# Layer 0's preparation in a four-layer network on one Trainium2 core: batch statistics from row tiles, another queue and layout for the first weights, per-channel factors through transposed rows, and a bias table split before it is spread

## The chip, the cores and the metric

The kernel runs on one core of a Trainium2 chip. A core has a matrix engine (TensorE, PE in the profile, its weight loads PEld), a vector engine (VectorE, DVE), a scalar engine (ScalarE, ACT), a general one (GpSimd, POOL) and a queue engine for transfers (SyncE, SP). Each runs its own instructions in the order in which they stand in its queue; semaphores order the engines against each other. SP, ScalarE and GpSimd can issue transfers (DMA) between the chip's memory and the on-chip memory. The metric is the device time of one execution in microseconds (us).

## The reference, cut to what matters

Four layers work on `x` of shape (4, 8, 512, 512), each as `x = x + layer(_gn(x))`, where `_gn` normalises over groups of planes. The change touches what is prepared for layer 0, a spiking attention block:

```python
T, B, N, D, H = (4, 8, 512, 512, 8)
def bn(x, g, b, m, v):
    return g * (x - m) * jax.lax.rsqrt(v + EPS) + b
q = heads(lif(bn(x @ Wq.T, bnq_g, bnq_b, bnq_m, bnq_v)))
k = heads(lif(bn(x @ Wk.T, bnk_g, bnk_b, bnk_m, bnk_v)))
v = heads(lif(bn(x @ Wv.T, bnv_g, bnv_b, bnv_m, bnv_v)))
scores = jnp.einsum('tbhnd,tbhmd->tbhnm', q, k) * scale
rel = pos[None, :] - pos[:, None] + (N - 1)
bias = bias_table[rel].transpose(2, 0, 1)
scores = scores + bias[None, None]
out = lif(einsum(scores, v) in token order)
out = out * gate_scale + gate_shift
out = lif(bn(out @ Wp.T, bnp_g, bnp_b, bnp_m, bnp_v))
```

`lif` steps a potential over the four time steps `t`, emits a spike where it reaches 1 and resets it. Layers 1 to 3 are convolutions of 13x13, 3x3 and 3x3.

## The kernel before

**Tiling.** Layer 0 works in 32 steps, one for each of 8 images and 4 time steps. A plane of 512 x 512 values is 1 MB; it is loaded in four transfers of 256 KB. `load_x` loads rows: four tiles of 128 partitions with 2 KB each, from six buffers (tag `x`). `load_quarters` loads the same plane into one tile `xq` for a transpose in blocks: each of its four transfers goes to 32 partitions, in pieces of 512 bytes; there is one buffer.

**Before the first step.** `load(0)` fetches `xq` of step 0, then `load_weights("v", nc.sync)` the weights `w_v` (1 MB, four transfers to 32 partitions each). `statistics` runs `bn_stats` (L431) over the two images of the first group: the first from `xq`, the second from rows (`xs`). `norm_of` combines them (L177 to L197) into a mean and a reciprocal deviation. `batch_norms` (L315 on) turns the batch norm's parameters into `a_half` and `c_half`, one value for each channel, laid along the partitions. Then `transpose` normalises `xq` in place (L618), transposes it (L480), and the projections begin (L499).

**Factors along the free axis.** The weights of v, k and the output are scaled by a factor for each output channel, which lies along the free axis. `along_free` brings it there: for each of four chunks it makes a diagonal matrix on VectorE (L336) and multiplies it by a matrix of ones on PE (L337). `prepare_in` uses it for v and k, `prepare_out` for the output's weights `wp`.

**Bias.** For each head the bias is a Toeplitz matrix. The kernel keeps it as three bf16 parts (`toep`), whose sum is the fp32 value, with 896 columns in 128 partitions. `prepare_bias` loads for each of 8 heads a table that is shifted by one element from partition to partition (L361, 448 KB), casts it reversed on ScalarE (L365), subtracts on VectorE (L366), casts (L367), subtracts on GpSimd (L368), and casts (L369). Its two scratch tiles have the tags `h_o` and `h_p`. The scratch of `bands1`, which prepares layer 1's bands (L726 to L757, `ps_band` at L741), takes tag `h_p` after it.

**Step loop.** Iteration `n` attends for step `n` and projects for step `n + 1`, in the order v, k, q (the q projection's potentials `v_q`, tag `v` with three buffers, go through ScalarE at L450). In iteration −1 only the projections of step 0 run, and then `prepare_bias`, `prepare_out`, `next_group` and `bands1`. Attention forms `ps_kv` (L515), for each of four head pairs `ps_a` (L527) and `ps_b` (L535, with `toep`), and then the potential `v_o` (L545 on ScalarE, L550 on VectorE). `project_out` (L562) uses the two parts of `wp`, which are made by L401, L405, L406 and L407.

**Order.** The program is written in one sequence. A planner puts the instructions into the engines' queues by priority in that sequence and by times that it expects, so a later instruction can stand ahead of an earlier one that has to wait. `tc.issue_after(op)` keeps what its block traces on `op`'s engine behind `op`. At run time each queue is strictly in order, and a transfer that has no free buffer or semaphore holds what stands behind it in its queue.

Of the kernel before, what the change touches and what calls it, by code (L numbers as in the profile page):

```python
# [34 lines left out]
F32 = mybir.dt.float32  # L35
# [8 lines left out]
P = 128  # L44
# [222 lines left out]
def layer0(  # L267
# [34 lines left out]


    def load_weights(n, engine):
        rows = i[f"wT_{n}"].rearrange("(q c a) e -> q a c e", c=NC, a=SQ)
        for q in range(P // SQ):
            engine.dma_start(wT[n][q * SQ : (q + 1) * SQ], rows[q])

    nc.scalar.dma_start(cols.rearrange("p a b -> p (a b)"), i["cols"])
    bn = cols[:, :16, :].rearrange("p (n s) c -> p n s c", s=4)  # L310
    ones = wpool.tile([P, P], F32, name="ones")
    nc.vector.memset(ones, 1.0)

    def batch_norms():

        neg_half = wpool.tile([P, 4, NC], F32, name="nh0")
        nc.vector.memset(neg_half, -0.5)
        nc.vector.tensor_scalar_add(a_half, bn[:, :, 3, :], EPS)
        nc.gpsimd.tensor_tensor(a_half, a_half, neg_half, op=ALU.pow)
        nc.vector.tensor_mul(a_half, a_half, bn[:, :, 0, :])  # L320
        nc.vector.tensor_scalar_mul(a_half, a_half, 0.5)
        c = c_half[:, :3, :]
        nc.vector.scalar_tensor_tensor(
            c, bn[:, :3, 2, :], -1.0, a_half[:, :3, :], op0=ALU.mult, op1=ALU.mult
        )
        nc.vector.scalar_tensor_tensor(
            c, bn[:, :3, 1, :], 0.5, c, op0=ALU.mult, op1=ALU.add
        )

    def along_free(cols):  # L330


        ps = ps_mm.tile([P, D], F32, tag="mm", name="ps_free")
        for c in range(NC):
            diag = work.tile([P, P], F32, tag="diag", name="diag", bufs=2)
            nc.vector.tensor_scalar_mul(diag, ident, cols[:, c : c + 1])  # L336
            nc.tensor.matmul(  # L337
                ps[:, c * P : (c + 1) * P], lhsT=ones, rhs=diag, start=True, stop=True
            )
        return ps  # L340

    def phases(x):
        return x.rearrange("p (v g) -> p g v", g=PH)

    def prepare_in(n):
        j = "qkvp".index(n)
        scale = along_free(a_half[:, j, :])
        for k in range(NC):
            nc.vector.tensor_mul(wT[n][:, k, :], wT[n][:, k, :], scale)
        return nc.scalar.mul(c_twice[n], along_free(c_half[:, j, :]), 2.0).ins  # L350

    def prepare_bias():


        n_u = toep[0].shape[2]
        table = i["table"]
        hankel = state.tile([P, 2, n_u], F32, tag="h_o", name="hankel")
        rest = state.tile([P, 2, n_u], F32, tag="h_p", name="rest")
        for h in range(H):
            src, r = hankel[:, h % 2, :], rest[:, h % 2, :]  # L360
            nc.scalar.dma_start(  # L361
                src, bass.AP(table.tensor, h * (2 * N - 1), [[1, P], [1, n_u]])
            )
            dst = [w[:, h, :] for w in toep]
            nc.scalar.copy(dst[0], src[:, ::-1])  # L365
            nc.vector.tensor_sub(r, src[:, ::-1], dst[0])  # L366
            nc.scalar.copy(dst[1], r)  # L367
            nc.gpsimd.tensor_sub(r, r, dst[1])  # L368
            nc.scalar.copy(dst[2], r)  # L369

    def load_out():
        wp32 = work.tile([P, NC, D], F32, tag="so", name="wp32")
# [3 lines left out]
    def prepare_out(wp32):  # L376
        gate_scale, gate_shift = cols[:, 16, :], cols[:, 17, :]

        shift = ps_1.tile([P, NC], F32, tag="misc", name="shift")
        for e in range(NC):  # L380
            for k in range(NC):
                nc.tensor.matmul(
                    shift[:, e : e + 1],
                    lhsT=wp32[:, k, e * P : (e + 1) * P],
                    rhs=gate_shift[:, k : k + 1],
                    start=k == 0,
                    stop=k == NC - 1,
                )
        c = c_half[:, 3, :]
        nc.vector.tensor_sub(c, shift, bn[:, 3, 2, :])  # L390
        nc.vector.tensor_mul(c, c, a_half[:, 3, :])
        nc.vector.scalar_tensor_tensor(c, bn[:, 3, 1, :], 0.5, c, op0=ALU.mult, op1=ALU.add)

        nc.scalar.mul(
            c_twice["p"].rearrange("p (g v) -> p g v", g=PH), phases(along_free(c)), 2.0
        )
        scale = work.tile([P, D], F32, tag="v", name="scale_p", bufs=3)
        nc.scalar.copy(scale, along_free(a_half[:, 3, :]))
        for k in range(NC):
            wp = work.tile([P, D], F32, tag="v", name="wp_k", bufs=3)  # L400
            nc.vector.scalar_tensor_tensor(  # L401
                wp.rearrange("p (g v) -> p g v", g=PH), phases(wp32[:, k, :]),
                gate_scale[:, k : k + 1], phases(scale), op0=ALU.mult, op1=ALU.mult,
            )
            nc.scalar.copy(wpT[0][:, k, :], wp)  # L405
            nc.vector.tensor_sub(wp, wp, wpT[0][:, k, :].bitcast(F32))  # L406
            nc.scalar.copy(wpT[1][:, k, :], wp)  # L407

    def load_x(b, t, name):
        got = []  # L410
        for c in range(NC):
            xt = xp.tile([P, D], F32, tag="x", name=f"{name}_{b}_{t}_{c}")
            nc.sync.dma_start(xt, x_in[t, b, c * P : (c + 1) * P, :])
            got.append(xt)
        return got
# [9 lines left out]
    def as_rows(xt):  # L425
        flat = xt.rearrange("p j f -> p (j f)")
        return [flat[:, c * D : (c + 1) * D] for c in range(NC)]
# [176 lines left out]
    def statistics(g, t, pair, xt):  # L604
        key = g, t
        if pair == 0:
            norms[key] = new_stats(g, t)
        count(xt, norms[key], pair)
        if pair == PAIR - 1:
            norms[key] = norm_of(g, t, norms[key])  # L610
# [12 lines left out]
    def load(n):  # L623
        if n <= last:
            xs[n] = load_quarters(*steps[n])
# [14 lines left out]
        image_bands(nc, bt, band, 0, r1[:, 0, 0:1], eye)  # L640
        return band, eye, x, bt

    load(0)
    load_weights("v", nc.sync)
    statistics(0, 0, 0, as_rows(xs[0]))
    statistics(0, 0, 1, load_x(1, 0, "xs"))
    batch_norms()
    for k in range(NC):
        transpose(0, k)
    with tc.issue_after(prepare_in("v")):  # L650
# [4 lines left out]
    for n in range(-1, last + 1):  # L655
        b, t = steps[max(n, 0)]
        if n >= 0:
            with tc.issue_after(did) if n == 0 else ExitStack():
                so = attend(spikes, t)
            residual = load_x(b, t, "xr")  # L660
            if n == last:
                head = start_layer1()
        if n + 1 <= last:
            spikes = new_spikes()
            g, j = divmod(n + 1, PAIR * T)
            if n >= 0:
                load(n + 2)
            if j == 2 and g > 0:
                norm1(g - 1, ps_1)
            if g == 0 and n >= 0 and n + 2 < T:  # L670
                statistics(0, n + 2, 0, as_rows(xs[n + 2]))
                statistics(0, n + 2, 1, load_x(1, n + 2, "xs"))
            if n >= 0:
                next_group(n)
        for a, name in enumerate("vkq"):
            for c in range(NC):
                if n + 1 <= last:
                    did = project_in(name, c, xns[n + 1], spikes, steps[n + 1][1])
                if (n, name, c) == (-1, "v", 0):
                    first += [prepare_in("k"), did, potentials[0]]  # L680
                    with ExitStack() as behind:
                        for op in first:
                            behind.enter_context(tc.issue_after(op))
                        load(1)
                        statistics(0, 1, 0, as_rows(xs[1]))
                        statistics(0, 1, 1, load_x(1, 1, "xs"))
                if n >= 0 and a < 2 and c % 2:
                    project_out(so, 2 * a + c // 2, residual[2 * a + c // 2], b, t)
                if a == 2 and c % 2:
                    transpose(n + 2, c // 2)  # L690
        if n + 1 <= last:
            del xns[n + 1]
        for k in range(2, NC):
            transpose(n + 2, k)
        if n < 0:
            with ExitStack() as behind:
                for op in first:
                    behind.enter_context(tc.issue_after(op))
                prepare_bias()
                prepare_out(load_out())  # L700
                next_group(n)
                bands1(tc, i, band1d, w_sum, eye, ps_mm, state)
            for name in "op":
                h_of[name] = state.tile([P, NC, N], F32, tag=f"h_{name}", name=f"h_{name}")
# [614 lines left out]
```

## Time and profile before

| what | value |
|---|---|
| median of 3 runs | 2932.97 us (2931.45 to 2935.19) |
| the profiled execution | 2934.12 us |
| its span, first to last instruction | 2932.3 us |
| PE busy | 2826.4 us (96%), 12,865 matmuls |
| VectorE busy | 2210.8 us (75%) |
| ScalarE busy | 551.0 us (19%) |
| GpSimd busy | 1036.6 us (35%) |
| read from and written to the chip's memory | 210.57 MB and 103.60 MB |

The profile gives for every instruction its start, its duration, its line in the kernel and what it waited for; times count from the start of the span. Its page shows the whole span in 40 slices of 73 us, with the busy share of each engine in tenths. Its other views can be cut to a stretch of time: busy time by stretch, instructions in order of time with the idle time ahead of each and what ended it, transfers by queue, and waits by engine. Busy times of PE are those of pipelined matmuls. "Granted clock" is the share of its full clock that PE was allowed.

### The profile page before, as it was taken

How to read it: one execution, taken by the hardware profiler on the slowest of the kernel's cores; microseconds unless marked ns; L12 is line 12 of the kernel's file. 1: busy time of each engine (PE TensorE's matmuls, PEld its weight loads, DVE VectorE, ACT ScalarE, POOL GpSimd, SP SyncE). 2: the span in 40 equal slices, each digit the busy share in tenths (PEclk: the TensorE clock that was granted, in tenths of full speed). 3: DMA queues.
4: the chain of work that ended last, by engine and by line, in shares of the span. 5: the costliest groups of instructions: out<-in, count | busy, mean ns of one | idle time of the engine just before them, and what ended most of it. 6: DMA issues, size and time to landing. Idle time of an engine off the chain costs nothing. (4 is left out here: it accounts for less than half of the span.)

```text
span 2932.3 us, 36617 instructions
## 1 busy us (share of the span) xinstructions
PE 2826.4 (96%) x12865; PEld 1302.0 (44%) x12865; DVE 2210.8 (75%) x3916; ACT 551.0 (19%) x860; POOL 1036.6 (35%) x1924
## 2 busy tenths in 40 slices
PE   6899999999999999999999999999999999589999
PEld 3454555554555544455455555455333333223334
DVE  7897788688779778868877886886655556887870
ACT  1300010011010001001000000110111111766664
POOL 3342233343234323323422433332211112676650
PEclk9899999999999999999999999999999999999999
DMA  7333322223222223222222122113878779698865
GB/s 182 100 81 80 73 59 66 72 71 78 64 66 66 73 76 70 59 66 66 73 66 51 45 59 51 52 44 87 224 194 222 207 200 242 145 212 214 221 171 147
DMA packets 323895, 322.10 MB, mean 110 GB/s; under 512 B 21431, under 2 KB 237183, under 8 KB 323599
## 3 DMA queue, kind: packets, MB, share of 16 engines
q1 hardware_dynamic: 261872, 237.39, 33.4%
q0 software_dynamic: 19776, 56.14, 6.0%
q10 hardware_dynamic: 42063, 26.23, 3.2%
q8 instruction: 101, 1.65, 0.3%
q14 instruction: 83, 0.68, 0.1%
HBM read 210.57 MB, written 103.60 MB: 107 GB/s over the span
## 5 line engine op out<-in xcount | busy, mean ns | idle before, releaser
L499 PE MATMUL ps_in<-w_v,xn 128*128 128x512 f32 x1024 | 459.2, 598 | 3.0 <-DVE xn L480 3.0
L499 PE MATMUL ps_in<-w_kq,xn 128*128 128x512 f32 x1024 | 450.1, 592 | 0.0
L815 PE MATMUL ps_conv<-x,bt 112*64 112x512 f32 x2048 | 445.0, 592 | 0.8 <-DVE v_p L467 0.8
L499 PE MATMUL ps_in<-xn,w_kq 128*128 128x512 f32 x1024 | 444.6, 592 | 0.0
L535 PE MATMUL ps_b<-toep,vtok 128*64 128x512 bf16 x3072 | 368.9, 384 | 1.0 <-DVE v_o L550 1.0
L475 POOL TENSOR_TENSOR h_v<-h_v,c_v 128x512 f32<-128x512 f32 x96 | 122.0, 1271 | 683.9 <-DVE h_v L474 658.2
L450 ACT ACTIVATE h_q<-v_q,c_half 128x512 f32<-128x512 f32 x96 | 69.2, 721 | 1473.6 <-DVE v_q L446 950.4
L584 POOL COPY x1s<-x1s 128x2 f32<-128x2 f32 (+1 forms) x1024 | 227.7, 277 | 272.3 <-DVE x1s L573 272.3
L562 PE MATMUL ps_out<-wp,so 128*128 128x512 f32 x1024 | 308.9, 444 | 0.0
L499 PEld LDWEIGHTS ps_in<-xn,w_kq 128*128 128x128 f32 x1024 | 194.3, 190 | 233.0 <-issue 223.2
L499 PEld LDWEIGHTS ps_in<-w_kq,xn 128*128 128x128 f32 x1024 | 194.2, 190 | 219.9 <-issue 204.7
L499 PEld LDWEIGHTS ps_in<-w_v,xn 128*128 128x128 f32 x1024 | 190.9, 191 | 218.4 <-issue 210.1
L815 PEld LDWEIGHTS ps_conv<-x,bt 112*64 112x64 f32 x2048 | 144.9, 135 | 290.2 <-issue 288.1
L1220 PE MATMUL ps_conv<-x,band_t 64*64 64x512 f32 x2040 | 251.4, 609 | 3.1 <-DVE band_t L1189 3.1
L535 PEld LDWEIGHTS <-vtok 128*64 128x64 bf16 x3072 | 176.0, 111 | 155.5 <-issue 7.0
L1083 POOL COPY u<-x 128x512 f32<-128x512 f32 (+1 forms) x172 | 211.7, 1266 | 91.8 <-issue 48.2
L562 PEld LDWEIGHTS ps_out<-wp,so 128*128 128x128 f32 x1024 | 192.6, 188 | 94.4 <-issue 58.1
L573 DVE SCALAR_TENSOR_TENSOR x1s<-v_p,xr 128x256 f32<-128x256 f32 x256 | 188.6, 777 | 13.1 <-DMA x<-x1s 2.3
L837 POOL DMA_DIRECT2D x<-xo x128 | 71.6, 566 | 314.0 <-ACT xo L822 299.7
L475 POOL TENSOR_TENSOR h_k<-h_k,c_k 128x512 f32<-128x512 f32 x96 | 123.3, 1284 | 135.9 <-DVE h_k L474 135.9
L822 ACT ACTIVATE xo<-ps_conv,off 128x512 f32<-128x512 f32 x128 | 87.9, 687 | 430.9 <-PE ps_conv L815 314.8
L1125 DVE SCALAR_TENSOR_TENSOR x<-ps_conv,inv,u 128x512 f32<-128x512 f32 (+1 forms) x172 | 121.3, 745 | 56.3 <-PE ps_conv L1118 29.0
(192 smaller groups left out, 3268.5 us busy)
## 6 DMA issues: line engine op xcount, KB each, us to landing
x<-x SPq DMA_DIRECT2D x64, 917.0 KB
x<-x SPq DMA_DIRECT2D x168, 256.0 KB
x<-x1s POOLq DMA_DIRECT2D x128, 262.0 KB, 2.7
xq<-in_x SPq DMA_DIRECT2D x128, 256.0 KB
xr<-in_x SPq DMA_DIRECT2D x128, 256.0 KB
out<-o SPq DMA_DIRECT2D x164, 192.0 KB
xs<-in_x SPq DMA_DIRECT2D x112, 256.0 KB
x<-xo ACTq DMA_DIRECT2D x128, 128.0 KB
```

The lines of the kernel that those rows point to most:

```text
L475: nc.gpsimd.tensor_add(h, h, c_twice[n])
L499: mm = nc.tensor.matmul(ps, lhsT=lhsT, rhs=rhs, start=k == 0, stop=k == NC - 1)
L535: nc.tensor.matmul(pb[two * DH : (two + 1) * DH, :], lhsT=v[:, c, h * DH : (h + 1) * DH], rhs=toep[z][:, h, u : u + N], start=c == 0 and z ...
L562: nc.tensor.matmul(ps, lhsT=so[:, k, c * P : (c + 1) * P], rhs=wpT[z][:, k, :], start=k == 0 and z == 0, stop=k == NC - 1 and z == 1,)
L573: nc.vector.scalar_tensor_tensor(own, v.rearrange("p (g v) -> p g v", g=PH)[:, two, :], 1.0, by_phase[:, two, :], op0=ALU.is_ge, op1=ALU.add,)
L584: nc.gpsimd.tensor_copy(x1[:, f, u : u + n], x1[:, fm, um - n + 1 : um + 1][:, ::-1])
L815: mm = nc.tensor.matmul(ps[q * M1 : (q + 1) * M1, :], lhsT=bt[:, z, :], rhs=xt[:, w0 : w0 + N_PS1, z : z + NV], start=z == 0, stop=z == SH ...
L822: nc.scalar.activation(xo[:, a, :], ps, AF.Identity, bias=off[:, t : t + 1])
L837: engine.dma_start(bass.AP(dst.tensor, dst.offset + (q * n_half * W1_OUT * B + b) * D + f * NV, [[B * D, W1_OUT], [W1_OUT * B * D, n_half] ...
L1083: nc.gpsimd.tensor_copy(u[:n_p, j, :].rearrange("p (v g) -> p v g", g=PH), x[:, j, :].rearrange("p (g v) -> p v g", g=PH),)
L1125: done["DVE"] = nc.vector.scalar_tensor_tensor(own, ps[:n_p, :], w["inv"][:n_p], u[:n_p, j, :], op0=ALU.mult, op1=ALU.add, accum_out=sums[ ...
L1220: mm = nc.tensor.matmul(ps[j][b * HALF : (b + 1) * HALF, :], lhsT=band[half, b, dx, :], rhs=x3[half, s0 + j, dx : dx + D], start=dx == 0, ...
```

## The change

Five things change. (1) `batch_norms` is traced first and returns its last operation. The statistics of both images of the first group come from row tiles, behind that operation on VectorE; `xq` of step 0 is traced after them. (2) The weights of v are loaded from ScalarE's queue and not from SP's, and each of the four transfers of any of these weights covers 128 partitions with 2 KB rather than 32 with 8 KB. (3) `along_free` takes rows that PE has transposed and ScalarE has copied (`as_rows_of`), and spreads them with a column of the identity, broadcast, as the stationary operand; the diagonals and the matrix of ones are gone. In `prepare_out` the scale is now traced ahead of `c`. (4) `split_bias` splits the table while it is compact, as 24 partitions of 341 values, on VectorE, and stores the three bf16 parts in the chip's memory. (5) `prepare_bias` loads each part, shifted by one element from partition to partition, for two heads at a time, and ScalarE copies it reversed into `toep`: 12 loads and 12 copies.

```diff
     def load_weights(n, engine):
-        rows = i[f"wT_{n}"].rearrange("(q c a) e -> q a c e", c=NC, a=SQ)
-        for q in range(P // SQ):
-            engine.dma_start(wT[n][q * SQ : (q + 1) * SQ], rows[q])
+        rows = i[f"wT_{n}"].rearrange("(q c a) e -> c q a e", c=NC, a=SQ)
+        for c in range(NC):
+            engine.dma_start(wT[n][:, c, :], rows[c])
...
+    def as_rows_of(cols):
+        n = cols.shape[1]
+        ps = ps_mm.tile([n, P], F32, tag="mm", name="ps_rows")
+        nc.tensor.transpose(ps, cols, ident)
+        rows = wpool.tile([4 * NC, P], F32, tag="rows", name="rows", bufs=2)
+        nc.scalar.copy(rows[:n], ps)
+        return rows[:n]
+
+    def along_free(rows, j):
+        n = rows.shape[0]
         ps = ps_mm.tile([P, D], F32, tag="mm", name="ps_free")
         for c in range(NC):
-            diag = work.tile([P, P], F32, tag="diag", name="diag", bufs=2)
-            nc.vector.tensor_scalar_mul(diag, ident, cols[:, c : c + 1])
+            at = NC * j + c
             nc.tensor.matmul(
-                ps[:, c * P : (c + 1) * P], lhsT=ones, rhs=diag, start=True, stop=True
+                ps[:, c * P : (c + 1) * P], lhsT=ident[:n, at : at + 1].to_broadcast([n, P]),
+                rhs=rows, start=True, stop=True,
             )
...
+    def split_bias():
+        n_e = n_h // 3
+        parts = tc.dram_tile([3, H * n_h], BF16, name="bias_parts")
+        src = state.tile([3 * H, n_e], F32, tag="h_o", name="bias_table")
+        nc.scalar.dma_start(src, bass.AP(i["table"].tensor, 0, [[n_e, 3 * H], [1, n_e]]))
+        part = state.tile([3 * H, 3, n_e], BF16, tag="h_p", name="bias_part")
+        for z in range(3):
+            nc.vector.tensor_copy(part[:, z, :], src)
+            if z < 2:
+                nc.vector.tensor_sub(src, src, part[:, z, :])
+        nc.scalar.dma_start(
+            bass.AP(parts.tensor, parts.offset, [[n_e, 3 * H], [H * n_h, 3], [1, n_e]]), part
+        )
+        return parts
+
+    def prepare_bias(parts):
+        for h in range(0, H, 2):
+            for z in range(3):
+                hankel = state.tile(
+                    [P, 2, n_u], BF16, tag="h_o" if (h + z) % 2 else "h_p", name="hankel"
+                )
+                nc.scalar.dma_start(
+                    hankel,
+                    bass.AP(
+                        parts.tensor, parts.offset + (z * H + h) * n_h, [[1, P], [n_h, 2], [1, n_u]]
+                    ),
+                )
+                nc.scalar.copy(toep[z][:, h : h + 2, :], hankel[:, :, ::-1])
...
+        scale = work.tile([P, D], F32, tag="v", name="scale_p", bufs=3)
+        nc.scalar.copy(scale, along_free(a_rows, 3))
 
         nc.scalar.mul(
-            c_twice["p"].rearrange("p (g v) -> p g v", g=PH), phases(along_free(c)), 2.0
-        )
-        scale = work.tile([P, D], F32, tag="v", name="scale_p", bufs=3)
-        nc.scalar.copy(scale, along_free(a_half[:, 3, :]))
+            c_twice["p"].rearrange("p (g v) -> p g v", g=PH), phases(along_free(as_rows_of(c), 0)), 2.0
+        )
...
-    load(0)
-    load_weights("v", nc.sync)
-    statistics(0, 0, 0, as_rows(xs[0]))
-    statistics(0, 0, 1, load_x(1, 0, "xs"))
-    batch_norms()
+    normed = batch_norms()
+    a_rows = as_rows_of(a_half.rearrange("p n c -> p (n c)"))
+    c_rows = as_rows_of(c_half[:, :3, :].rearrange("p n c -> p (n c)"))
+    load_weights("v", nc.scalar)
+    with tc.issue_after(normed):
+        for pair in range(PAIR):
+            statistics(0, 0, pair, load_x(pair, 0, "xs"))
+        load(0)
+        bias_parts = split_bias()
```

## The prediction

> **What bounds the kernel now.** First the page's slices, then a table of stretches (columns: stretch, its length, busy time and instructions of PE, PEld, DVE, ACT, POOL, then granted clock, DMA share, GB/s).
>
> ```profile
> PE   6899999999999999999999999999999999589999
> ```
>
> ```profile
> 0.00:30.00 30.00, 5.92 (x20) 4.71 (x20) 14.52 (x42) 1.88 (x2) 4.96 (x9) 1.00 1.00 230
> 30.00:78.00 48.00, 45.61 (x116) 21.16 (x117) 42.77 (x70) 13.00 (x15) 20.12 (x13) 1.00 0.55 150
> 78.00:98.00 20.00, 18.70 (x116) 11.50 (x114) 17.45 (x29) 12.07 (x16) 6.71 (x4) 0.74 0.66 152
> 98.00:114.00 16.00, 5.12 (x21) 3.20 (x23) 13.84 (x28) 6.48 (x12) 0.84 (x1) 0.62 0.37 95
> 114.00:130.00 16.00, 16.00 (x78) 7.39 (x73) 12.12 (x30) 4.03 (x7) 2.49 (x3) 0.95 0.20 57
> 130.00:400.00 270.00, 267.73 (x1063) 135.69 (x1062) 222.84 (x378) 18.50 (x28) 99.45 (x209) 1.00 0.28 71
> ```
>
> From 114 us on PE is full, so what the change is worth is the PE time it gives back in the first 114 us. PE loses time in two places: before its first projection, and between 78 and 114 us (1.30 + 10.88 us idle, and at clocks 0.74 and 0.62 another 18.70 × 0.26 + 5.12 × 0.38 = 6.8 us). Nothing in the change can return more than about 30 + 2 + 19 us.
>
> The start, in order of time, and SP's longest wait for a transfer:
>
> ```profile
> 21.64 1.36 DVE L431 BATCH_NORM_STATS2 st<-xs 128x6 f32<-128x512 f32 x2 [4.50 <-DMA xs<-in_x]
> 24.70 0.17 DVE L177 TENSOR_REDUCE gsum_x<-st 128x1 f32<-128x16 f32 x1
> 30.18 5.35 PE L499 MATMUL ps_in<-w_v,xn 128*128 128x512 f32 x8 [3.00 <-DVE xn L480]
> ```
>
> ```profile
> SPq L413 <- DMA w_kq<-in_wT_k: 6.7, 3, 5.5
> ```
>
> Statistics wait for rows of pair 1, and SP issues those behind k's weights. From the last statistic to the first projection is a fixed chain, 30.18 − 24.70 = 5.5 us. The DMA view, microsecond 15 to 16 (weights), then 21 to 22 (rows):
>
> ```profile
> DMA packets 111, 0.20 MB, mean 205 GB/s; under 512 B 11, under 2 KB 11, under 8 KB 111
> q10 hardware_dynamic: 111, 0.20, 106.7%
> ```
>
> ```profile
> DMA packets 210, 0.39 MB, mean 387 GB/s; under 512 B 21, under 2 KB 21, under 8 KB 210
> q1 hardware_dynamic: 210, 0.39, 105.0%
> ```
>
> Packets of 2 KB in both, but weights go to 32 partitions in one transfer and rows to 128.
>
> The second hole, on PE and then on ScalarE:
>
> ```profile
> 97.32 0.62 PE L535 MATMUL ps_b<-toep,vtok 128*64 128x512 bf16 x3
> 105.26 1.91 PE L741 MATMUL ps_band<-bands 13*52 13x128 f32 x8 [7.32 <-DMA bands<-in_w]
> 109.83 0.56 PE L180 MATMUL gps_x<-gsum_x,avg 128*128 128x1 f32 x2 [2.66 <-DVE gsum_x L177]
> 111.92 0.58 PE L535 MATMUL ps_b<-toep,vtok 128*64 128x512 bf16 x1 [0.95 <-DVE v_o L550]
> ```
>
> ```profile
> 98.87 0.94 ACT L369 CAST toep<-rest 128x896 bf16<-128x896 f32 x1 [0.80 <-POOL rest L368]
> 107.98 0.59 ACT L545 ACTIVATE v_o<-ps_a 128x512 f32<-128x512 f32 x1
> ```
>
> The bias split ends at 99.81. Only then is its buffer (tag h_p) free for the bands' scratch, whose transfers land at 105.26; and attention's first v_o stands in ScalarE's queue behind it and behind the output weights' casts.
>
> **What the Trainium skill says.** "SBUF — State Buffer", section Door 1: 0 to 31 partitions reach 8 of 16 ports (about 218 GB/s), 128 all of them (436). The trace agrees: 205 against 387. The same page, Who interferes with whom: a VectorE instruction with two SBUF inputs or in a two-port mode blocks against a GpSimd one that reads SBUF. The trace agrees: the k spikes of L504 take 0.38 to 0.41 us alone, and 1.69 and 2.10 us at 60.13 and 69.62, beside POOL's subtraction L368 (59.65, 69.15). "ScalarE: Activation LUTs", What ACT_TABLE_LOAD costs: 186 ns + 0.833 ns an element. The casts agree: 0.93 us computed for 896, 0.94 measured. "TensorE: Matmul & The Clock Gate", What's actually happening: too little activity halves the clock; here it follows the 32 one-column matmuls L382 and the idle stretch.
>
> **Part 1, loads and statistics.** Off SP: four w_v transfers. Onto SP: four more row transfers (1.05 MB), and xq is now behind the rows. Onto ScalarE's queue, ahead of everything but cols: four w_v (4 × 0.44 us of issue), then the table's load (33 KB) and the store of the split (49 KB). The weights move at the rows' rate, since a transfer now spans 128 partitions. From the first data at 2.0 us: constants 1 us; w_v and 8 rows 3.15 MB at 0.39 MB/us, 8.1; xq 1.05 MB at 0.205, 5.1: 16.2 us. Rows 7 and 8 need a buffer (six of tag x), free when two statistics ran after batch_norms ended (7.9 us), so k's weights can share the engines: 1.05/0.39 = 2.7 us more, q's as much again. Bounds for the last row 16.2 and 21.6; I take k's alone, 18.9, less 0.4 for constants that run beside the first rows: 18.5. Then 0.7 us of statistics, then 5.5: first projection at 24.7, **5.5 us earlier** (bounds 2.4 and 7.8).
>
> VectorE could forbid it: from 7.9 us eight statistics (8 × 0.62), w_v's scaling (4 × 0.62) and the split, sized from the 0.42 us copy and the 0.67 us subtraction of 512 columns: 3 × 0.3 + 2 × 0.45 = 1.8. That is 9.3 us, done by 17.2, under the transfers. The store waits on VectorE; behind it in ScalarE's queue may stand c_v and the k and q weights. Nobody needs those before 38 us.
>
> **Part 2, rows instead of diagonals.** Gone: 24 diagonals of 0.28 us. Matmuls stay 48, of 16 or 12 rows rather than 128; priced the same (0.275). Added: three transposes (0.28) and three ScalarE copies of 128 columns (0.3); the first two pairs lie before 10 us, under the loads. At k's preparation (34.9 to 38.3, 41.7 to 43.2) PE alternates with the diagonals; without them **2.0 us** come back: idle 0.60 and 0.65, plus the gaps inside.
>
> **Part 3, the bias.** Gone: 24 casts × 0.94 = 22.6 us of ScalarE, 8 × 1.08 of VectorE (two at 1.74), 8 × 1.9 of POOL, with the blocking above. Added: 12 loads of 459 KB for 8, and 12 copies of 1792 columns, 0.186 + 0.833 × 1.792 = 1.68 us each, 20.2 in all; four more issues of 0.34 us on ScalarE's queue, under its waits for the loads (without that cover 1.4 us). The buffers alternate by z alone, so the sequence is p, o, p, p, o, p: eight of twelve use h_p, one at a time. A turn is load plus copy. The load at 68.20 had its data by 71.1 and its reader could go at 71.48: 3.3 us; the turn is 5.2. From c_k (43.45 now, about 36 then) the chain ends at 36 + 2 (first load beside wp) + 8 × 5.2 = **80 us** in place of 99.8. The page shows no 1792-byte packets from odd addresses: at 3.3 us if nothing changes, at 4.4 if they go at half rate (0.459 MB at 0.4 and 0.2 MB/us differ by 1.1), so 80 to 88. I take 80.
>
> PE's projections now end at 78.4; minus 5.5, 2.0 and nothing else, 71. Its way to the third head pair (shift 4.2, kv 1.9, 48 ps_b at 0.12 each, as 24 in 2.78 us at 121.16, to 0.21, as 20 in 4.17 at 87.82) reaches 84 or later, so pairs 0 to 2 are there and the last just is. Scratch free at 80, bands at 84.5: the 7.32 us wait goes. What is late next: v_o, behind the casts L405 and L407 (8 × 0.62), which no longer wait for c's chain, as scale_p comes first. I leave 4 us idle and half the clock loss (L382 stays): 12.2 − 4 + 3.4 = **11.6 us** (bounds 3 and 17).
>
> **Sum.** 5.5 + 2.0 + 11.6 = 19.1. The profiled execution took 2934.1 (span 2932.3 and 1.8 around it); 2915.0. The median of runs, 2932.97, is 1.1 lower, so 2914 to 2915.
>
> **Rivals.**
> - The stall only moves: the planner leaves v_o behind casts and ps_band, and PE still stands from about 90. For: v_o sits 0.5 us behind L407 today. Against: those casts' source was VectorE's backlog, now 20 us lighter. The second hole gives 3: 2934.1 − 10.5 = 2923.6. Chance 0.16.
> - The start gives little: k's and q's weights both pass the rows, as k's did today. First projection 28, a gain of 2.2: 2934.1 − 15.8 = 2918.3 if the rest holds, 2926.9 with the former. Chance 0.10.
> - The change doesn't do what it says: w_v lands behind other transfers, VectorE waits for the table ahead of the statistics, and the end moves under 0.2%, about what a measurement of this kernel can tell from no change (5.9 us). Chance 0.08.
> - **Slower**: ScalarE's in-order queue at the hankel copies. Behind every late load stand h_q (which holds one of three v buffers), the wp casts and v_o. For: eight serial turns on one buffer, and 5.5 MB read for 3.7 beside xs, xr and wp on the same engines. Against: the DMA share is 0.55 there. It decides from a turn of 8 us: 36 + 2 + 64 = 102, v_o then at today's 108. At 9.5 us, v_o at about 120: 12 later, 2946. Chance 0.08.
>
> **Numbers.** The main case keeps 0.58 and its own range 2905 to 2923. Below 2902 (nearly all 19 us of the second hole and a start at 22.4) 0.07; above 2932 about 0.12. Faster by over 0.2% 0.84, within 0.08, slower 0.08.
>
> **What would show it.** First L499 near 24.7; w_v near 390 GB/s; no idle of PE at L337; last toep copy near 80, 1.68 us each; ps_band without its 7 us; L504 never over 1 us in that stretch. Wrong if turns take over 6 us, if rows land after 21.6, or if PE is not full by 100 us.

## The result and the profile after

The changed kernel is slower, by 0.5%. Its median is 2947.79 us (five runs, 2946.7 to 2953.14) against 2932.97 of the kernel before (five runs, 2931.45 to 2935.19): ratio 1.0053, interval [1.0042, 1.0065]. Its profiled execution took 2947.97 us, with a span of 2946.2.

The page's row for PE in 40 slices of the span shows the first two slices emptier than before:

```profile
PE   3899999999999999999999999999999999679999
```

The same table of stretches as in the prediction (stretch, length, busy time and instructions of PE, PEld, DVE, ACT, POOL, then granted clock, DMA share, GB/s):

```profile
0.00:30.00 30.00, 4.48 (x18) 3.66 (x18) 8.83 (x24) 2.29 (x4) 4.41 (x8) 1.00 0.55 159
30.00:78.00 48.00, 23.63 (x61) 11.77 (x62) 21.89 (x48) 7.33 (x5) 4.94 (x5) 0.85 0.73 183
78.00:98.00 20.00, 20.00 (x47) 8.87 (x46) 15.71 (x28) 6.64 (x4) 6.62 (x6) 0.93 0.61 195
98.00:114.00 16.00, 16.00 (x81) 10.42 (x79) 11.88 (x23) 7.20 (x9) 0.00 (x0) 0.81 0.80 201
114.00:130.00 16.00, 10.24 (x66) 5.84 (x63) 9.90 (x20) 9.14 (x13) 0.00 (x0) 0.82 0.32 89
```

Before 130 us PE is idle for 55.7 us (each length less its busy time, summed); before the change it was 38.7. The 30 to 78 us stretch, formerly full but for 2.4 us, now lacks 24.4. The hole of 78 to 114 us is gone and a smaller one stands at 114 to 130. The DMA share of the first 30 us is 0.55, down from 1.00: the engines that move data have become idler, while everything waits for data.

PE in order of time (start, duration, and in brackets the idle time ahead and what ended it):

```profile
38.92 5.79 PE L523 MATMUL ps_in<-w_v,xn 128*128 128x512 f32 x8 [5.58 <-DVE xn L504]
...
75.52 0.59 PE L180 MATMUL gps_x<-gsum_x,avg 128*128 128x1 f32 x2 [16.63 <-DVE gsum_x L177]
...
104.37 3.63 PE L406 MATMUL shift<-cols,wp 128*128 128x1 f32 x32
...
125.82 1.91 PE L770 MATMUL ps_band<-bands 13*52 13x128 f32 x8 [5.20 <-DMA bands<-in_w]
```

The first projection stands at 38.92, not at 24.7 and not at the 30.18 of before. A new hole of 16.63 us lies in the middle of step 0's projections: PE waits for the statistics of step 1. `ps_band` waits 5.20 us where 7.32 were to vanish.

Who is late is read on VectorE, in the same kind of view:

```profile
27.90 0.69 DVE L455 BATCH_NORM_STATS2 st<-xs 128x6 f32<-128x512 f32 x1 [2.90 <-DMA xs<-in_x]
29.14 0.69 DVE L455 BATCH_NORM_STATS2 st<-xs 128x6 f32<-128x512 f32 x1 [0.55 <-DMA xs<-in_x]
...
36.77 1.35 DVE L642 TENSOR_SCALAR xq<-xq,gmean_x,grstd_x 128x2048 f32<-128x2048 f32 x1 [3.24 <-DMA xq<-in_x]
...
72.32 2.47 DVE L455 BATCH_NORM_STATS2 st<-xq 128x6 f32<-128x512 f32 x4 [16.79 <-DMA xq<-in_x]
```

The last two statistics of step 0 waited for their rows and ran at 27.90 and 29.14 us; the later one ended 7 us ahead of the normalisation at 36.77. What ended the wait at 36.77 is the plane `xq` of step 0, and 16.79 us of VectorE's idle time ahead of the statistics at 72.32 end with another `xq`. So rows are late, and planes later still, both times. SP's queue shows why (line, transfer waited for: us in total, times, longest):

```profile
SPq L446 <- DMA w_v<-in_wT_v: 13.6, 2, 10.4
...
SPq L437 <- DMA w_kq<-in_wT_k: 11.5, 2, 6.7
...
SPq L446 <- DMA w_kq<-in_wT_q: 8.1, 2, 4.3
```

L446 issues the quarters of `xq`, L437 the rows. Both stand behind transfers of weights. `xq` needs nothing of `w_v`; why its transfer has to wait for that one is not in the trace (a semaphore that both use would do it, which is a guess). The DMA view of the microsecond 14 to 15, in which weights alone move:

```profile
DMA packets 49, 0.10 MB, mean 98 GB/s; under 512 B 1, under 2 KB 1, under 8 KB 49
q10 hardware_dynamic: 49, 0.10, 26.2%
```

98 GB/s, and 26.2% of 16 engines' time, which is that of 4.2 engines. Before, the weights moved at 205 GB/s on 106.7%. The edit that was to double their rate has halved it, and what stopped was not the engines' speed but their number: 98 GB/s over 4.2 is 23 GB/s an engine, 205 over 16 is 13.

### The profile page after: what moved, and what is told of

It is laid out like the page before. It is cut to its first block, busy times and chain, and to the rows that moved or that the text cites. A ratio compares the mean times of both kernels' runs of the same rounds, so it can differ in the third digit from the quotient of the medians.

```text
span 2946.2 us, 36585 instructions
## 1 busy us (share of the span) xinstructions
PE 2826.1 (96%) x12868; PEld 1304.8 (44%) x12868; DVE 2196.8 (75%) x3888; ACT 549.2 (19%) x851; POOL 1016.0 (34%) x1916
## 5 line engine op out<-in xcount | busy, mean ns | idle before, releaser
L523 PE MATMUL ps_in<-w_v,xn 128*128 128x512 f32 x1024 | 458.9, 599 | 5.6 <-DVE xn L504 5.6
L523 PE MATMUL ps_in<-w_kq,xn 128*128 128x512 f32 x1024 | 452.5, 595 | 0.0
L523 PE MATMUL ps_in<-xn,w_kq 128*128 128x512 f32 x1024 | 444.6, 592 | 0.0
L499 POOL TENSOR_TENSOR h_v<-h_v,c_v 128x512 f32<-128x512 f32 x96 | 121.8, 1269 | 710.7 <-DVE h_v L498 664.2
L586 PE MATMUL ps_out<-wp,so 128*128 128x512 f32 x1024 | 309.0, 444 | 0.0
L523 PEld LDWEIGHTS ps_in<-xn,w_kq 128*128 128x128 f32 x1024 | 194.3, 190 | 233.0 <-issue 221.3
L523 PEld LDWEIGHTS ps_in<-w_kq,xn 128*128 128x128 f32 x1024 | 195.2, 191 | 221.3 <-issue 206.9
L523 PEld LDWEIGHTS ps_in<-w_v,xn 128*128 128x128 f32 x1024 | 191.3, 191 | 222.6 <-issue 211.6
L586 PEld LDWEIGHTS ps_out<-wp,so 128*128 128x128 f32 x1024 | 192.6, 188 | 94.4 <-issue 57.6
L499 POOL TENSOR_TENSOR h_k<-h_k,c_k 128x512 f32<-128x512 f32 x96 | 122.0, 1271 | 138.2 <-DVE h_k L498 138.2
L574 DVE SCALAR_TENSOR_TENSOR v_o<-ps_b,v_o 128x512 f32<-128x512 f32 x128 | 88.4, 691 | 97.3 <-PE ps_b L559 97.3
```

Of the source, the lines that this page charges most:

```text
L499: nc.gpsimd.tensor_add(h, h, c_twice[n])
L523: mm = nc.tensor.matmul(ps, lhsT=lhsT, rhs=rhs, start=k == 0, stop=k == NC - 1)
L574: nc.vector.scalar_tensor_tensor(w, pb, 0.5, w, op0=ALU.mult, op1=ALU.add)
L586: nc.tensor.matmul(ps, lhsT=so[:, k, c * P : (c + 1) * P], rhs=wpT[z][:, k, :], start=k == 0 and z == 0, stop=k == NC - 1 and z == 1,)
```

## The experiments

Three moments of each profiled execution carry the comparison: A, the first projection (L499 before, L523 after); S, the `shift` matmuls (L382, L406), which follow step 0's projections; O, the end of attention's first output projection (`ps_out`, L562, L586), by which 16 of the 32 matmuls of step 1's v projection have run in every kernel. "Chain" runs from the first to the end of the last operation that writes `toep`. A ratio is to the runs of the kernel before on the same chip at the same time, whose medians lay between 2931.62 and 2933.75 us.

| kernel | median us | ratio to before | A | A to S | S to O | O | chain |
|---|---|---|---|---|---|---|---|
| before | 2932.97 | | 30.18 | 48.22 | 51.97 | 130.37 | 48.98 to 99.81 |
| after | 2947.79 | 1.0053 [1.0042, 1.0065] | 38.92 | 65.45 | 44.02 | 148.39 | 59.09 to 121.79 |
| e1_old_layout | 2923.10 | 0.9968 [0.9956, 0.9981] | 27.64 | 46.28 | 54.34 | 128.26 | 46.09 to 109.72 |
| e2_before_new_layout | 2945.99 | 1.0041 [1.0028, 1.0055] | 38.07 | 57.85 | 50.24 | 146.16 | |
| e3_before_bias | 2931.22 | 0.9995 [0.9986, 1.0003] | 31.90 | 47.46 | 48.22 | 127.58 | 50.71 to 101.27 |
| e5_full_rows | 2919.94 | 0.9958 [0.9945, 0.9970] | 23.91 | 46.18 | 46.80 | 116.89 | 36.08 to 90.71 |
| e6_turns | 2911.38 | 0.9929 [0.9917, 0.9942] | 28.84 | 46.13 | 39.95 | 114.92 | 40.93 to 85.23 |
| e7_before_full_rows | 2923.03 | 0.9974 [0.9962, 0.9986] | 25.49 | 48.19 | 51.95 | 125.63 | 44.33 to 95.09 |
| e8_full_rows_old_bias | 2917.50 | 0.9953 [0.9939, 0.9966] | 26.47 | 46.75 | 46.18 | 119.40 | 39.81 to 88.71 |
| e9_v_full_rows | 2938.63 (one run) | | 26.05 | 69.29 | 43.76 | 139.10 | |
| e11_outer_2 | 2969.41 (one run) | | 45.36 | | | | |
| e12_old_start | 2912.65 | 0.9928 [0.9911, 0.9944] | 25.00 | 46.86 | 38.80 | 110.66 | 38.05 to 78.41 |
| e13_again | 2922.54 (one run) | | 27.57 | 45.95 | 45.96 | 119.48 | 39.84 to 92.77 |

From O to the end of the program an execution takes 2794 to 2804 us whatever the edit, so single differences of O can be off by up to 10 us against the medians. The medians decide what an edit is worth, the moments where it lies.

**Is it the form of the weights' transfers?** Three runs. The first takes the changed kernel and gives it back the old form; the second gives the new form to the kernel before; the third takes the changed kernel and gives its transfers 128 plain rows, for which the weights lie in memory in another order.

```diff
 e1_old_layout, on the changed kernel:
-        rows = i[f"wT_{n}"].rearrange("(q c a) e -> c q a e", c=NC, a=SQ)
+        rows = i[f"wT_{n}"].rearrange("(q c a) e -> q a c e", c=NC, a=SQ)
-            engine.dma_start(wT[n][:, c, :], rows[c])
+            engine.dma_start(wT[n][q * SQ : (q + 1) * SQ], rows[q])
 e2_before_new_layout, on the kernel before: the reverse
```

> The changed kernel with the old form of the weight loads (four transfers to 32 partitions with 8 KB each), still from ScalarE's queue. Theory A: weights at 0.2 MB/us again, first projection at 25 to 29 us, the hole at 59 us gone or under 3 us, total 2914 to 2926 us; a few us slower than with full rows, as w_v takes 5 us rather than 2.7. Theory B: within 3 us of the changed kernel, 2944 to 2950.

> The kernel before with only the new form of the weight loads (four transfers with outer dimension 4), v still from SP. Theory A: w_v at 0.1 MB/us takes 10.5 us, k's and q's weights 21 us on the same few DMA engines; first projection at 36 to 45 us instead of 30.2, total 2940 to 2955 us. Theory B: as the kernel before or faster, 2928 to 2936 us, since a transfer now covers 128 partitions.

Measured: e1_old_layout 0.9968 [0.9956, 0.9981], e2_before_new_layout 1.0041 [1.0028, 1.0055]. So this one edit turns a gain into the loss: it costs 2947.79 − 2923.10 = 24.7 us with the rest of the change around it, and 13.2 without (2945.99 against 2932.84 for the kernel before on the same chip). PE of e2_before_new_layout shows both signs of it, in a kernel that has nothing else of the change:

```profile
38.07 5.84 PE L499 MATMUL ps_in<-w_v,xn 128*128 128x512 f32 x8 [3.00 <-DVE xn L480]
...
67.92 0.58 PE L180 MATMUL gps_x<-gsum_x,avg 128*128 128x1 f32 x2 [7.54 <-DVE gsum_x L177]
```

The start is 7.9 us later than before, and the wait for step 1's statistics is there too, 7.54 us long.

```diff
 e5_full_rows, on the changed kernel (memory order of in_wT_q, _k, _v to match):
-        rows = i[f"wT_{n}"].rearrange("(q c a) e -> c q a e", c=NC, a=SQ)
+        rows = i[f"wT_{n}"].rearrange("(c p) e -> c p e", p=P)
```

> The changed kernel, with one thing different: the weights of q, k and v lie in memory in such an order that each of their four transfers is a plain block of 128 rows, which goes to 128 partitions with a single outer dimension of 128, where the changed kernel's has an outer dimension of 4. Order of all queues unchanged. Theory A (a weight transfer with outer dimension 4 runs on 4 of the 16 DMA engines, moves 0.1 MB/us, and holds up the rows and xq behind it): weights at 0.35 to 0.4 MB/us, first projection at 23 to 27 us instead of 38.9, the 16.6 us hole at 59 us gone, first output projection near 120 us instead of 146, total 2912 to 2922 us. Theory B (the loss is in the rest: four more row transfers, xq behind them, the split's load and store in ScalarE's queue, the hankel loads): first projection later than 35 us, total above 2940.

Measured 2919.94, 0.9958 [0.9945, 0.9970]. The instructions stand in the queues as in the changed kernel; packets have 2 KB in both and go to the same 128 partitions. Its DMA view of the microsecond 16 to 17 (k's weights) and its PE:

```profile
DMA packets 198, 0.36 MB, mean 358 GB/s; under 512 B 23, under 2 KB 23, under 8 KB 198
q10 hardware_dynamic: 198, 0.36, 100.7%
```

```profile
23.91 5.87 PE L523 MATMUL ps_in<-w_v,xn 128*128 128x512 f32 x8 [4.59 <-DVE xn L504]
...
94.85 1.91 PE L770 MATMUL ps_band<-bands 13*52 13x128 f32 x8 [8.53 <-DMA bands<-in_w]
```

All 16 engines at 22 GB/s each, and the first projection at 23.91, near the 24.7 of the prediction, once the transfer does what it was said to do. The second line is the part that still fails; it is taken up below.

**What sets the number of engines?** The changed kernel's transfer has the access pattern [4, 32, 512]: four blocks of 32 rows, 128 rows apart. The next run cuts each transfer into two of [2, 32, 512].

```diff
-            engine.dma_start(wT[n][:, c, :], rows[c])
+            for q in range(0, P // SQ, 2):
+                engine.dma_start(wT[n][q * SQ : (q + 2) * SQ, c, :], rows[c, q : q + 2])
```

> The changed kernel, each weight transfer cut into two with outer dimension 2 (64 partitions, 128 KB). If the outer dimension sets the number of DMA engines: two engines, 0.05 MB/us and 13% of the 16 while the weights run alone, first projection after 45 us, total above 2965 us. If 0.1 MB/us comes from the scattered rows in memory, or from the number of partitions in another way: 0.1 to 0.2 MB/us still, total 2940 to 2952 us.

Measured 2969.41, A at 45.36. The DMA view, microsecond 20 to 21 (`w_v`):

```profile
DMA packets 25, 0.05 MB, mean 49 GB/s; under 512 B 1, under 2 KB 1, under 8 KB 25
q10 hardware_dynamic: 25, 0.05, 13.1%
```

13.1% of 16 is 2.1 engines, at 49 GB/s. A share of 26.2% could also be 16 engines that are each mostly idle; the trace's records of single packets tell the two apart. In the microseconds 13 to 15 of the changed kernel four weight packets are in flight for 84% of the time, in 19 to 22 of e11 two for 90%, and a packet of 2 KB takes 85 ns in both (the median); in e5, from 16.2 to 17 us, it takes 87 with 16 or more in flight for 78% of the time. An outermost dimension of 2, 4 and 128 gives 2, 4 and 16 engines. The Trainium skill states this rule, "DMA: Bandwidth & Descriptors", section Why a DMA increments its semaphore by 16 and not by 1: the engine count is the largest number up to 16 that divides the slowest dimension that is not 1 of both access patterns. These three runs agree with it. So does the old form, with 32 partitions outermost: it used all 16 engines for a quarter of the partitions, so the number of partitions is not what sets it. Nor is it the blocks in memory, as e11 reads the same blocks of 32 rows as the changed kernel, on half the engines. What held the old form at 205 GB/s no run here tests; the prediction took it for the ports, and the trace has its 2 KB packets at 170 ns each (median, 15 to 16 us).

**Which of the weights made the hole in the middle?** Plain rows for v alone; k and q keep the new form.

> The kernel with full rows for v's weights only; k's and q's keep the form with outer dimension 4. If v's weights made the late start and k's and q's made the hole inside the projections: first projection at 24 to 30 us, then a wait of 8 to 18 us for the statistics of step 1, first output projection at 126 to 140 us. If the hole only followed from the late start: no wait over 3 us, first output projection at 114 to 119 us.

Measured 2938.63. PE of e9_v_full_rows:

```profile
26.05 5.81 PE L526 MATMUL ps_in<-w_v,xn 128*128 128x512 f32 x8 [4.74 <-DVE xn L507]
...
66.87 0.59 PE L180 MATMUL gps_x<-gsum_x,avg 128*128 128x1 f32 x2 [20.82 <-DVE gsum_x L177]
```

The start comes back with v's weights. The hole stays and is even 20.82 us long, so it belongs to k's and q's: their transfers are not needed early, but step 1's rows and its `xq` stand behind them.

**What are the other parts worth?** The bias alone on the kernel before; the plain rows alone on the kernel before; and the changed kernel with plain rows and the old bias preparation.

```diff
 e3_before_bias, on the kernel before:
+    bias_parts = split_bias()            # after batch_norms()
-                prepare_bias()
+                prepare_bias(bias_parts)
 e7_before_full_rows, on the kernel before: e5's edit, and nothing else
 e8_full_rows_old_bias, on e5_full_rows: e3's edit taken out
```

> The kernel before with only the bias part of the change: the table split compact on VectorE and stored, then 12 loads and 12 copies; weights, statistics and diagonals as before. Theory A: first projection within 3 us of 30.2, the second hole shorter by 6 to 12 us, total 2921 to 2928 us. Theory B (the hankel loads are a cost of their own): turns of 6 us or more on tag h_p and the rows of step 1 late, total 2935 to 2948.

> The kernel before with only full rows for the weights of q, k and v (outer dimension 128), v still from SP. By theory A w_v takes 2.7 us rather than 6, k's weights 2.7 rather than 5.3: first projection at 24 to 28 us instead of 30.2, total 2926 to 2931 us. If the gain of e5 were all in the new order of loads and not in the weights' rate: 2931 to 2935.

> The kernel with full rows (e5), and the old bias preparation (24 casts, subtractions on VectorE and GpSimd). First projection 22 to 25 us. If the bias part is worth what the second hole shrank in e5 (49.7 to 44.5 us from the end of the projections to the first output projection): 2923 to 2928 us, and VectorE's spikes blocked beside GpSimd again. If the bias part gives nothing here, as it gave 1.6 us alone in e3: 2918 to 2922 us.

The bias part by itself: 0.9995 [0.9986, 1.0003], nothing that can be measured, and a total between those of the two theories. With plain rows the intervals with the bias part (0.9945 to 0.9970) and without it (0.9939 to 0.9966) lie on each other. The table's last column says why in part. From its first to its last operation the old chain takes 50.8, 50.8 and 48.9 us (before, e7, e8), the new one 50.6, 54.6 and 52.9 (e3, e5, e13), and 63.6 and 62.7 in e1 and the changed kernel, where the weights move more slowly (in e1 `h_q`, ahead of two of the copies, alone waits 13.08 us for `v_q`). The casts and subtractions are gone, but the chain is not shorter. And O follows its end: 30.6, 30.5 and 30.7 us later with the old preparation (before, e7, e8), 26.3, 26.2, 26.7 and 26.6 later with the new one as it stands in the change (e3, e5, e13, after; only e1, at 18.5, falls out). So with plain rows the new form gains some 4 us behind the chain and loses 4 to 6 in it. In e3 nothing is lost in the chain, and A to O is 4.5 us shorter in its profile than before; why its median is only 1.6 us lower stays open.

Plain rows alone, e7, bring 0.9974 [0.9962, 0.9986]: A is 4.7 us earlier, and the stretches from A to O are as before. Its 2923.03 is less than the 2926 to 2931 that were expected, and what A doesn't explain of the gain lies after O, in the scatter named above.

**Why is the bias chain not shorter?** In order of time on ScalarE of e5_full_rows:

```profile
61.59 1.69 ACT L393 COPY toep<-hankel 128x1792 bf16<-128x1792 bf16 x1 [0.72 <-DMA hankel<-bias_parts]
...
68.67 1.67 ACT L393 COPY toep<-hankel 128x1792 bf16<-128x1792 bf16 x1
...
74.51 1.69 ACT L393 COPY toep<-hankel 128x1792 bf16<-128x1792 bf16 x1 [2.53 <-DMA hankel<-bias_parts]
...
83.36 1.69 ACT L393 COPY toep<-hankel 128x1792 bf16<-128x1792 bf16 x1 [2.37 <-DMA hankel<-bias_parts]
...
89.03 1.68 ACT L393 COPY toep<-hankel 128x1792 bf16<-128x1792 bf16 x1 [1.12 <-DMA hankel<-bias_parts]
```

The first line is the second copy of the last of four pairs, for which both buffers were loaded at once. The four after it come one at a time, 5.7 to 8.9 us apart. By the tags four of the twelve turns are h_o's and went into the pairs, so these four are all h_p's, and h_o lies empty meanwhile. If the buffers' turns are the cause, a tag that changes with every copy must end the chain earlier:

```diff
-                    [P, 2, n_u], BF16, tag="h_o" if (h + z) % 2 else "h_p", name="hankel"
+                    [P, 2, n_u], BF16, tag="h_o" if (3 * h // 2 + z) % 2 else "h_p", name="hankel"
```

> The kernel with full rows (e5), and the two scratch tiles of the bias loads used strictly in turn (p, o, p, o) instead of p, o, p, p, o, p. If the chain of loads and copies sets when the bands' scratch comes free: in e5 the copies run in 4 pairs and 4 singles from 36.1 to 90.7 us, 7.6 us a turn; six pairs at 7.6 end at 36 + 46 = 82 or earlier (76 at 6.6), the 8.5 us wait of ps_band falls under 2 us, first output projection at 107 to 111 us instead of 114.6, total 2911 to 2917 us. If that wait is only a place where PE would wait for something else anyway (v_o behind the casts): another wait takes its place, 2918 to 2922 us.

Measured 2911.38, 0.9929 [0.9917, 0.9942], 8.6 us below e5_full_rows (7.3 when each is set against its own runs of the kernel before), with intervals that just don't touch. The chain takes 44.3 us where it took 54.6. Its last copy, on ScalarE, and then PE of e6_turns:

```profile
83.54 1.69 ACT L393 COPY toep<-hankel 128x1792 bf16<-128x1792 bf16 x1 [0.52 <-DMA hankel<-bias_parts]
```

```profile
91.73 1.07 PE L770 MATMUL ps_band<-bands 13*52 13x128 f32 x8
```

`ps_band` has no wait left, and S to O falls to 39.95. With e12_old_start below, this is the fastest version of the study: 20.2 us under the kernel before on the same chip (2931.62) and 36.4 under the changed one's median. Against e8_full_rows_old_bias on the same chip the new bias form in strict turns gains 6.1 us (2917.50 to 2911.38, and no run of the one reaches into the other's).

**The order of the start, and its scatter.** e12_old_start is e6_turns with the loads and statistics in the order of the kernel before: `xq` first, v's weights from SP, the first image's statistics from `xq` (`batch_norms` stays ahead of them). e13_again is e5_full_rows once more.

```diff
 e12_old_start, on e6_turns:
-    load_weights("v", nc.scalar)
+    load(0)
+    load_weights("v", nc.sync)
     with tc.issue_after(normed):
-        for pair in range(PAIR):
-            statistics(0, 0, pair, load_x(pair, 0, "xs"))
-        load(0)
+        statistics(0, 0, 0, as_rows(xs[0]))
+        statistics(0, 0, 1, load_x(1, 0, "xs"))
```

> The kernel with full rows and strict turns (e6), with the old start: xq first, v's weights from SP behind it, the first image's statistics from xq. If the new order of the start has a worth of its own (e8 is 5.5 us faster than e7, of which the rows in place of diagonals are 2): 2913 to 2917 us. If the start is only bound by the bytes and their rate, and one plane less to load makes up for the rest: 2907 to 2912 us.

> The kernel with full rows (e5) once more, unchanged, for one profile: e5 and e6 have the same queues up to 30 us, and first projections at 23.9 and 28.8 us. If the start scatters by itself: anywhere from 23 to 30 us. If e6's late start came from its edit: within 1 us of 23.9.

e12_old_start: 0.9928 [0.9911, 0.9944], an interval that lies on that of e6_turns. The new order of the start, the first item of the change, is worth nothing measurable once the weights move on all engines. e13_again has its first projection at 27.57 where the same program had 23.91 on another chip, so a single A means little within some 4 us; why it scatters stays open.

## Why the prediction was wrong, step by step

**The start, "the weights move at the rows' rate, since a transfer now spans 128 partitions".** This step failed, and it alone decides the sign. They moved at 98 GB/s, not 387. The argument looked at the partitions that receive the data and not at how the transfer is divided among the engines: 32 rows in each of four blocks, hence four engines. The sign of it stood in the diff, `c q a e` with q = 4 outermost, and the prediction's page on ports is silent on it. First projection 38.92 for 24.7 (bounds 22.4 and 27.8), and the last row at 29 us, where "wrong" was set at 21.6. With transfers of plain rows the same queues gave 23.91 and 27.57 (e5, e13), within the bounds, and e6's 28.84 just outside. That e5 comes so near to 24.7 is luck in part. Its last statistic ended at 15.83, where the prediction has 19.2, and the chain from there, fixed at 5.5 us in the prediction, took 7.9, because `xq` came after the statistics were ready (8.9 in the changed kernel, from 29.99 to 38.92). VectorE of e5_full_rows:

```profile
21.77 1.34 DVE L642 TENSOR_SCALAR xq<-xq,gmean_x,grstd_x 128x2048 f32<-128x2048 f32 x1 [2.25 <-DMA xq<-in_x]
```

**What stands behind a transfer.** The prediction counted k's weights as 2.7 us and said that nobody needs them before 38 us. True, and beside the point: step 1's rows and `xq` wait in SP's queue for the weights' transfers to end (11.5 and 8.1 us in the view above). This is the 16.63 us hole, shown to come from k's and q's form by e9 (hole kept with v mended) and e5 (gone with all three). Of the +18.0 us at O, the start is +8.7, the projections +17.2, and the rest of the way −8.0. The two spans differ by 13.9 only; the other 4 us come late, in layers 2 and 3. The granted clock differs there in both directions (0.86 at 2670 to 2690 us before and 1.00 after, 18 us later; but 0.74 at 2570 to 2590 before and 0.62 after); the cause stays open.

**Part 2, 2.0 us.** Right. A to S fell from 48.22 to between 45.95 and 46.86 in the six kernels with rows and undisturbed loads (e1, e5, e6, e8, e12, e13), and stayed 48.19 and 47.46 in e7 and e3, which have the diagonals. It does more than was reckoned: the bias chain, which waits for c_k, begins 33.4 to 34.0 us ahead of S where rows are used (e5, e6, e8, e12, e13), and 28.7 to 29.4 where diagonals are (before, e3, e7). e12 has the old order of the start, so this goes with the rows. The exception is e1, with rows and 27.8, where ScalarE waited 8.21 us for other loads ahead of its first copy.

**The bias, 11.6 us.** The copies were priced right (1.68; measured 1.67 to 1.69), the work of VectorE and POOL on the bias went, and the spikes of L504 (L528 in the changed kernel) took at most 0.43 us in that stretch, as forecast. The term that failed is the turn, 5.2 us. In e5, from the first copy's end (37.77) to the last one's (90.71), seven more turns took 52.9 us, 7.6 each; the prediction reckoned eight, 41.6 us, from 38, and an end at 80. "Wrong if turns take over 6 us" came true. While the copies run in pairs a turn took 6.9 to 9.5 us: a load's issue stands in ScalarE's queue behind the other buffer's copy, and the load took 4 to 7 us from issue to reader. The single turns at the end took 5.8, 8.9 and 5.7 us. The shortest load, 3.95 us (85.08 to 89.03), is still above the 3.3 that was taken from the old one. One copy (68.67) also stood behind `h_q`, which waited 4.77 us for `v_q`.

S to O gained 5.2 us in e5, but e8, with the old preparation, gained 5.8, and `ps_band` waits only 0.41 us there: its chain begins 4.0 us further ahead of S than before and is 1.9 us shorter. So half of the 11.6 came without the new form, most of it with the earlier start of the chain that goes with part 2's rows, and the new form as it stands added nothing. With strict turns S to O gains 51.97 − 39.95 = 12.0 us. That is close to the 11.6, but only 6.2 of it (46.18 − 39.95) are the new form's, and they need an edit that the change doesn't have.

**The sum.** e5 does all three terms as the prediction described them: 12.9 us below the kernel before on the same chip (2932.84), where 19.1 were forecast. e6, which mends the turn alone, comes to 20.2. That this is near 19.1 is luck in part: e8, without the new bias form, is already 14.1 us below (2917.50 against 2931.62), where the first two terms make 7.5, and the strict turns add 6.1, where the third is 11.6.

**The rivals.** "Slower" got 0.08 by another mechanism, the in-order queue at the hankel copies with a turn of 8 us or more. It did not cause the loss: the turn is 8.7 us in the changed kernel and 8.9 in e1, and e1, with a chain that ends as late as 109.72, is faster than before. It was right that the turn is long and that v_o waits for it: in the changed kernel the first v_o ran at 125.68, behind the last copy. The rival that "the start gives little" saw the weights as passing the rows, but not that they could be slower than before. No rival had a transfer that gets slower, though the edit rewrites the loads of three weights; the start's term, given as a gain of 2.4 to 7.8 us, should have been left open towards a loss.

## What to carry to other kernels

When a transfer's access pattern is rewritten, look at its outermost dimension before its packet size and its partitions: 4 blocks of 32 rows ran on 4 engines, at a quarter of the rate of 128 rows with the same bytes to the same partitions. Read a DMA view by its two numbers together: here a low rate with a low share of the engines meant too few engines (98 GB/s, 26.2%), and a low rate with a full share something else (205 GB/s, 106.7%). Where buffers take turns, write out the sequence of tags over all the loops: `(h + z) % 2` with h in steps of two gives one buffer eight of twelve turns, and with the turns as they stood the new bias form gained nothing measurable.

## What was not expected of the hardware

- Engines taken by outermost dimension 2, 4, 128: 2.1, 4.2 and 16 of 16, at 49, 98 and 358 GB/s, 22 to 23 GB/s an engine; a packet of 2 KB took 85 to 87 ns in all three. The old form, 8 KB to each of 32 partitions, kept 16 engines busy at 13 each, with 170 ns a packet.
- A slow transfer holds others that have idle engines to run on. While `w_v` moved at 26.2% of the engines, SP waited 10.4 us for it before the first quarters of `xq`.
- One program's first projection came at 23.91 and 27.57 us in two executions, on two chips.
